# Local attention on one Trainium2 core: probabilities turned by VectorE in 32 by 32 blocks, the weighted state in four row groups of 32 keys, the previous key block by a shift in SBUF

## The chip, the cores and the metric

The kernel runs on one core of one Trainium2 chip. The metric is the device time of one execution in microseconds (us), as a median of several runs. Engines are named as in the profile: PE is TensorE (matrix products), PEld its weight loads, DVE is VectorE, ACT is ScalarE, POOL is GpSimd, and SP (SyncE) issues the DMAs. All data is float32.

## The reference

The reference is a two-block transformer on 16 sequences of 256 tokens and 128 channels. The change lies in one part of it: six layers of *local* attention with 16 heads of 64 channels, each followed by a gated feed-forward net (FFN). A window of 32 queries sees its own 32 keys and the 32 keys of the window before:

```python
def look(t):
    p = jnp.pad(t, ((0, 0), (0, 0), (1, 0), (0, 0), (0, 0)))
    return jnp.concatenate([p[:, :, :nw], p[:, :, 1:]], axis=3)
bk2, bv2 = (look(bk), look(bv))
...
sim = jnp.einsum('bhwie,bhwje->bhwij', bq, bk2) * QK_SCALE
sim = jnp.where(mask, -jnp.finfo(sim.dtype).max, sim)
attn = jax.nn.softmax(sim, -1)
out = jnp.einsum('bhwij,bhwje->bhwie', attn, bv2)
```

The keys before the first window are zeros and masked. Around it are a linear attention block ahead and a global attention block behind, which the change leaves alone.

## The kernel before, in words

The program has three stages. The first (linear attention) and the third (global attention) are not touched. The middle stage holds the six local layers; its first projection starts at 269 us, its first scores at 306 us, its last scores at 3444 us.

**Data.** Two sequences (512 tokens) make a *unit*; there are 8 units. The state of a unit lies with channels on partitions and tokens along the row (`zs`). The kernel does not form the values V: it weights the *state* by the probabilities (128 channels for every head) and then multiplies by the product of the V and output weights of that head (`wvo`). For that product the state must also lie with tokens on partitions: `upright` (L804) transposes it on PE, copies it on ACT (L813) and stores it to a DRAM buffer `rows` that has 32 zero rows ahead (L815); `windows` (L819) loads it back as `xw`, so that partitions 64·par to 64·par+63 hold the 64 keys of one window (L825, 8 loads for a unit).

**Steps.** The stage is one loop of 192 steps (`n`, L1065) and some more that drain it; step n handles two pairs of heads of one unit, so that a unit takes four steps, but each operation of a step belongs to an older step (its lag is in the code: scores `n - 4`, division `n - 5`, transposition `n - 6`, weighting `n - 9`, merging `n - 10`). The order of all instructions on PE, DVE, ACT and POOL is that of the Python program (`manual_schedule`, L1062): each engine works through its own list in that order. In a step, PE does in turn

1. `merging` (L942): 16 products of weighted state and `wvo`,
2. in odd steps a small transposition for key norms (L781, then DVE copies `rkT`, L783),
3. `flipped` (L902): 8 transpositions of the probabilities (L906); DVE copies each four of them from PSUM to `prT` (L911), so that keys lie on partitions,
4. in every fourth step `upright`, and parts of an FFN (`go_on(behind)`),
5. in even steps `norms_sum` (L729), whose result ACT copies (`n2`, L738),
6. `weighted` (L913): 8 products of `xw` (64 keys x 128 channels, held as weights) and `prT` (64 keys x 256 columns), in two rounds of two PSUM buffers; within a round two row groups of PE (partitions 0 to 63 and 64 to 127) work at once, each into a buffer of its own; DVE and ACT copy each buffer to `zx` (L934, L936),
7. `scores` (L858): 64 small products in 64 x 32 tiles, into separate `sim` buffers,
8. the projections (L705).

After the scores DVE finds row maxima (L870, L872), ACT computes 16 exponentials (L880) and puts the mask into the next `sim` buffers (L844), and DVE applies the rotary tables (L710, L713); POOL adds, scales and divides (L721, L802, L898).

**PSUM.** `bank()` (L58) hands out four buffers `mm` of one bank each, strictly in turn. So the first write to a buffer waits until the last reader of the *fourth buffer before it* is done. Projections, transpositions, norms, FFN parts and `weighted` all share this ring of four; `merging` and `scores` have their own.

**Four kinds of step.** Which FFN part falls into a step depends on n modulo 4:

- n = 4k, the *gate step*: `upright`, three gate products (L1004), their Gelu on ACT (L1006, with a table load), `norms_sum`; `weighted` does the last quarter of its unit.
- n = 4k+1, the *value step*: DVE adds the merged result to the state (L955), `rkT`, three value products (L1014) that DVE multiplies with the gates (L1018); `weighted` does the first quarter, which reads the `prT` that `flipped` finished in this same step.
- n = 4k+2, the *closing step*: the FFN's mean (L968), its output product (L1027), a row of small products (L977), `norms_sum`.
- n = 4k+3, the *plain step*: `rkT`, four transpositions (L994), which DVE multiplies in (L995, then L996).

Of the kernel before, what the change touches and what calls it, by code (L numbers as in the profile page):

```python
# [10 lines left out]
F32 = mybir.dt.float32  # L11
# [7 lines left out]
B, L, D = 16, 256, 128  # L19
NU = B // 2  # L20
U = 2 * L
DEPTH = 6
INNER = 1024
NP = INNER // 128
WIN = 32
# [19 lines left out]
def adaln_kernel(  # L45
# [25 lines left out]
    def work(tag, shape=(128, 512), bufs=None):  # L71
        if stage.get("flat"):
            t = stage["flat"].tile([128, 512], F32, tag="flat", name=tag)
            if len(shape) == 4:
                t = t.rearrange("p (a b c) -> p a b c", a=shape[1], b=shape[2])
            return t
        kw = {} if bufs is None else {"bufs": bufs}
        return stage["pool"].tile(list(shape), F32, tag=tag, name=tag, **kw)
# [521 lines left out]
    with ExitStack() as es:  # L600
# [24 lines left out]

        ks = [persistent(f"k{j}", (128, 2, PAD + L)) for j in range(8)]

        rows = [dr.tile([2, PAD + L, D], F32, tag=f"rows{j}", name=f"rows{j}") for j in range(2)]
        zero = work("zero")[0:PAD, 0:D]
        nc.vector.memset(zero, 0.0)  # L630
        for home in rows:
            for s in range(2):
                nc.sync.dma_start(home[s, 0:PAD, :], zero)
        rope = lc.tile([128, 2, 2, L], F32, tag="rope", name="rope")
        nc.sync.dma_start(rope, io["c_rope"].rearrange("p (j a) t -> p j a t", j=2))

# [164 lines left out]
            k = ks[m % 8][:, :, PAD:]  # L801
            nc.gpsimd.tensor_tensor(k, k, two(kn), ALU.mult)  # L802

        def upright(u, home):  # L804

            pt = bank()
            for t in range(4):
                s, c = t // 2, PAD + 128 * (t % 2)
                nc.tensor.transpose(
                    pt[:, t * 128 : (t + 1) * 128], zs[u][:, s, c : c + 128], ident  # L810
                )
            xt = work("xt").rearrange("p (s h d) -> p s h d", s=2, h=2)
            nc.scalar.copy(xt.rearrange("p s h d -> p (s h d)"), pt)  # L813
            for s in range(2):
                nc.sync.dma_start(  # L815
                    home[s, PAD : PAD + L, :].rearrange("(h p) d -> p h d", p=128), xt[:, s]
                )

        def windows(s, home):  # L819


            xw = atile("xw", (128, 8, 128))
            for r in range(0, 128, WIN):
                t0 = r % (2 * WIN)
                nc.sync.dma_start(  # L825
                    xw[r : r + WIN],
                    home[s, t0 : t0 + L, :].rearrange("(w p) d -> p w d", p=WIN),
                )
            return xw

# [66 lines left out]
                    prf, prf, rsum[:, x].unsqueeze(2).to_broadcast([128, 8, 64]), ALU.mult  # L899
                )  # L900

        def flipped(p, x, pr, prT):  # L902

            pt = bank()
            for st in range(4):
                nc.tensor.transpose(  # L906
                    pt[:, st * 128 : (st + 1) * 128],
                    pr[:, x, st].rearrange("p h k -> p (h k)"),
                    ident,
                )  # L910
            nc.vector.tensor_copy(prT[:, p + x, :], pt)  # L911

        def weighted(j, xw, prT):  # L913

            zx = atile("zx", (128, 2, NP, 128), 1)
            for k in (2 * j, 2 * j + 1):
                pz = [bank(), bank()]
                for w in range(2):
                    for par in range(2):
                        r = slice(64 * par, 64 * par + 64)  # L920
                        nc.tensor.matmul(  # L921
                            pz[par][:, w * 256 : (w + 1) * 256],
                            xw[r, (2 * k + w) % 8, :],
                            prT[r, :, 64 * k + 32 * w : 64 * k + 32 * w + 32],
                            start=True,
                            stop=True,
                            skip_group_check=True,
                        )
                for par in range(2):
                    c0 = 64 * (k % 2)  # L930
                    dst = zx[:, par, :, c0 : c0 + 64].rearrange("p a (w q) -> p w a q", w=2)
                    src = pz[par].rearrange("p (w a q) -> p w a q", w=2, a=NP)
                    if par:
                        nc.vector.tensor_copy(dst, src)  # L934
                    else:
                        nc.scalar.copy(dst, src)  # L936
            return zx

        def merging(j, zx, vo, py):
# [125 lines left out]
        while n < N + 10 or behind:  # L1065
# [19 lines left out]
            if 0 <= n - 6 < N:  # L1085
                i, u, p = place(n - 6)
                if p == 0:
                    prTs[i, u] = atile("prT", (128, NP, 512))
                pr = prs.pop(n - 6)
                for x in range(2):  # L1090
                    flipped(p, x, pr, prTs[i, u])
            for s, lag in ((0, 8), (1, 10)):
                v, r = divmod(n - lag, QS)
                if r == 0 and 0 <= v < DEPTH * NU:
                    if s == 0:
                        upright(v % NU, rows[v % 2])
                    xws[v, s] = windows(s, rows[v % 2])
            go_on(behind)
            if 0 <= n - 5 < N:
                divided(prs[n - 5], ssum)  # L1100
# [6 lines left out]
                n2 = norms_sum([squares.pop(m) for m in range(2 * n - 4, 2 * n)])  # L1107
            v, r = divmod(n - 9, QS)
            if 0 <= v < DEPTH * NU:
                zxs[v, r] = weighted(r, xws[v, r // 2], prTs[v // NU, v % NU])  # L1110
            go_on(behind)
            if sims:
                m = 2 * (n - 4)
# [506 lines left out]
```

## Time and profile before

| | |
|---|---|
| median of 3 runs | 4091.11 us (4088.63 to 4092.11) |
| span of the profiled execution | 4089.6 us, 1.5 us under the median |
| PE, DVE, ACT, POOL busy, share of the span | 94%, 72%, 68%, 65% |
| part of the middle stage, 306 to 1900 us: PE, DVE, ACT, POOL busy | 1507.7, 1197.6, 1153.0, 1137.1 of 1594 us |
| granted TensorE clock, 306 to 3460 us | 0.99 to 1.00 |
| median time from scores to scores, ending in the gate, value, closing, plain step | 17.69, 17.00, 17.75, 13.15 us |

The profile is one execution. Its groups give for each line of the program how often an operation ran, how long it was busy and what ended the idle time ahead of it; the chain of waits follows the end back from instruction to what released it; the timeline lists instructions in order. Busy time of PE is counted from start to modelled end, so neighbouring matrix products overlap in it, and a PE that is shown busy may still be waiting between two products. A float32 product is two records of PE ("x16" for 8 products), a transposition is one.

### The profile page before, as it was taken

The numbers are of one execution on the slowest core, as the hardware profiler recorded it, in microseconds if no ns is written. First come the engines' busy times: TensorE is split into PE (matmuls) and PEld (weight loads), VectorE is DVE, ScalarE is ACT, GpSimd is POOL, SyncE is SP. The second block draws the span as 40 slices with busy tenths as digits, with TensorE's granted clock in tenths as the row PEclk, the third lists the DMA queues.
The fourth block names the chain that finished last, engine by engine and source line by source line (L and its number), as shares of the span: only waits on it lengthen the run. The fifth ranks groups of instructions, "written<-read, shape, count | busy, mean of one in ns | idle before, by whom it ended". The sixth has DMA issues, their size and how long they took to land.

```text
span 4089.6 us, 117058 instructions
## 1 busy us (share of the span) xinstructions
PE 3824.8 (94%) x44534; PEld 2533.5 (62%) x44534; DVE 2944.4 (72%) x6006; ACT 2797.5 (68%) x9683; POOL 2653.6 (65%) x3374
## 2 busy tenths in 40 slices
PE   7877899999999999999999999999999999799998
PEld 4534666666666666666666666666666666455554
DVE  6756777777777777777777777777777775476664
ACT  4536777777777777677777777776777776366665
POOL 6437777767776777677776777777777665255453
PEclk9878999999999999999999999999999999899999
DMA  1334454445545445454554444454545443200000
GB/s 42 42 83 118 121 126 115 123 118 128 126 124 127 117 122 125 117 127 113 128 131 121 121 123 116 123 130 120 127 107 131 115 118 79 63 1 6 9 6 9
DMA packets 316617, 408.82 MB, mean 100 GB/s; under 512 B 48745, under 2 KB 212632, under 8 KB 316056
## 3 DMA queue, kind: packets, MB, share of 16 engines
q1 hardware_dynamic: 316056, 401.33, 39.6%
q8 instruction: 353, 5.78, 0.6%
q14 instruction: 208, 1.70, 0.1%
HBM read 178.26 MB, written 21.56 MB: 49 GB/s over the span
## 4 chain that ended last, share of the span: by engine, by line
PE 53%; DVE 16%; ACT 16%; issue 6%; POOL 5%; DMA 2%; SPq 1%; ACTq 0%; DVEq 0%; POOLq 0%
PE mm L921 8%; ACT pr L880 7%; PE y L942 6%; PE mm L705 6%; PE sim L858 6%; DVE sent L710 3%; PE mm L729 3%; PE mm L1027 3%; ACT sq L708 2%; PE mm L1014 2%; PE mm L1398 2%; DVE mx L870 2%; PE mm L906 2%; PE sim L1325 2%; DVE k L713 2%
## 5 line engine op out<-in xcount | busy, mean ns | idle before, releaser
L880 ACT ACTIVATE pr<-sim,nb,rq 128x64 f32<-128x64 f32 x3072 | 1229.2, 453 | 366.9 <-DVE nb L872 307.5
L880 ACT ACTIVATION_READ_ACCUMULATOR pr<-sim,nb,rq 128x1 f32 x3072 | 783.1, 255 | 0.0
L942 PEld LDWEIGHTS y<-zx,wvo 128*128 128x128 f32 x6144 | 715.8, 192 | 93.0 <-issue 88.3
L802 POOL TENSOR_TENSOR k<-k,kn 128x512 f32<-128x512 f32 x384 | 483.7, 1274 | 435.9 <-DMA kn<-rkh 434.4
L705 PE MATMUL mm<-z,wqk 128*128 128x512 f32 x1536 | 710.3, 604 | 13.4 <-DMA wqk<-in_L_ffn_Wqkv_dram 7.9
L942 PE MATMUL y<-zx,wvo 128*128 128x128 f32 x6144 | 717.9, 275 | 2.2 <-ACT zx L936 1.8
L721 POOL TENSOR_TENSOR q<-q,got 128x512 f32<-128x512 f32 x384 | 488.5, 1272 | 300.4 <-DMA got<-sent 173.2
L710 DVE SCALAR_TENSOR_TENSOR sent<-mm,vec,rope 128x512 f32<-128x512 f32 x768 | 571.0, 743 | 117.4 <-ACT sq L708 109.9
L934 DVE COPY zx<-mm 128x512 f32<-128x512 f32 x384 | 255.3, 674 | 375.0 <-PE mm L921 374.5
L708 ACT ACTIVATE sq<-mm 128x512 f32<-128x512 f32 x768 | 475.6, 619 | 30.9 <-PE mm L705 29.5
L721 POOL TENSOR_TENSOR k<-k,got 128x512 f32<-128x512 f32 x384 | 496.4, 1293 | 0.0
L705 PEld LDWEIGHTS mm<-z,wqk 128*128 128x128 f32 x1536 | 281.9, 192 | 328.5 <-issue 252.5
L921 PE MATMUL mm<-prT,xw 64*128 64x256 f32 x3072 | 452.5, 401 | 11.6 <-ACT n L738 6.4
L921 PEld LDWEIGHTS mm<-prT,xw 64*128 64x128 f32 x3072 | 326.7, 188 | 179.9 <-DVE rsum L893 38.6
L898 POOL TENSOR_TENSOR pr<-pr,rsum 128x512 f32<-128x512 f32 x384 | 392.3, 1043 | 14.0 <-PE mm L1004 7.4
L936 ACT COPY zx<-mm 128x512 f32<-128x512 f32 x384 | 227.0, 596 | 248.9 <-PE mm L921 248.4
L870 DVE TENSOR_REDUCE mx<-sim 128x8 f32<-128x512 f32 x384 | 263.1, 685 | 138.7 <-PE sim L858 137.9
L1368 POOL TENSOR_TENSOR pr<-pr,rsum 128x256 f32<-128x256 f32 (+1 forms) x256 | 205.1, 832 | 242.2 <-DVE rsum L1366 218.2
L858 PEld LDWEIGHTS sim<-k,q 64*32 64x32 f32 x24576 | 264.3, 106 | 80.9 <-issue 56.4
L858 PE MATMUL sim<-k,q 64*32 64x64 f32 x24576 | 299.5, 227 | 11.8 <-POOL k L802 6.5
L1354 ACT ACTIVATE pr<-lg,nm 128x128 f32<-128x128 f32 (+1 forms) x512 | 226.3, 443 | 117.3 <-DVE nm L1343 109.4
L713 DVE SCALAR_TENSOR_TENSOR q<-mm,vec,rope 128x512 f32<-128x512 f32 x384 | 284.5, 741 | 0.0
(253 smaller groups left out, 6244.7 us busy)
## 6 DMA issues: line engine op xcount, KB each, us to landing
got<-sent SPq DMA_DIRECT2D x1536, 128.0 KB
kn<-rkh SPq DMA_DIRECT2D x768, 128.0 KB
xw<-rows SPq DMA_DIRECT2D x384, 128.0 KB
rows<-xt SPq DMA_DIRECT2D x96, 128.0 KB
wqk<-in_L_ffn_Wqkv_dram SPq DMA_DIRECT2D x48, 128.0 KB
bhome<-brow SPq DMA_DIRECT2D x1, 3072.0 KB
wv<-in_L_ffn_Wqkv_dram SPq DMA_DIRECT2D x12, 256.0 KB
wo<-in_L_ffn_Wo_dram SPq DMA_DIRECT2D x12, 256.0 KB
```

What stands on the lines that cost most here:

```text
L705: nc.tensor.matmul(pp, wqk[:, j, :], xs, start=True, stop=True)
L708: nc.scalar.activation(sq, pp, AF.Square)
L710: nc.vector.scalar_tensor_tensor(two(sent[:, j, :]), two(pp), scale, tab[1], ALU.mult, ALU.mult)
L713: nc.vector.scalar_tensor_tensor(r, two(pp), scale, tab[0], ALU.mult, ALU.mult)
L721: nc.gpsimd.tensor_tensor(r, r, two(got[:, j, :]), ALU.add)
L802: nc.gpsimd.tensor_tensor(k, k, two(kn), ALU.mult)
L858: nc.tensor.matmul(sims[par][32 * c : 32 * c + 32, c0 : c0 + 64], q[r, s, t0 : t0 + 32], k[r, s, t0 : t0 + 64], start=False, stop=True, sk ...
L870: nc.vector.tensor_reduce(mx, sim.rearrange("p (b k) -> p b k", b=8), AX.X, ALU.max)
L880: nc.scalar.activation(pr[:, x, st, par, :], sims[par][:, b * 64 : (b + 1) * 64], AF.Exp, bias=nbs[par][:, b : b + 1], scale=rn[:, par, b ...
L898: nc.gpsimd.tensor_tensor(prf, prf, rsum[:, x].unsqueeze(2).to_broadcast([128, 8, 64]), ALU.mult)
L921: nc.tensor.matmul(pz[par][:, w * 256 : (w + 1) * 256], xw[r, (2 * k + w) % 8, :], prT[r, :, 64 * k + 32 * w : 64 * k + 32 * w + 32], star ...
L942: nc.tensor.matmul(py[:, j * 128 : (j + 1) * 128], vo[:, h, :], zx[:, h % 2, h // 2, :], start=(h == 0), stop=(h == 2 * NP - 1), skip_grou ...
```

## The change

The probabilities are no longer transposed on PE. One VectorE instruction turns the two pairs of a step at once, in blocks of 32 by 32, from SBUF to SBUF. In each block of 32 partitions the 32 queries of a window become 32 keys, either of the window's own block or of the block before. `weighted` therefore works on 32 keys at a time: four row groups (one for each window of a 128-token tile, c = 0 to 3), each with two products that are added up in PSUM (b = 0 the block before, b = 1 the own block), 128 channels by 512 columns. All four `mm` buffers are taken together, one for each row group. The number of products (8), of buffers taken (4) and of copies (4) in a step stays the same. The upright state stays in SBUF (`own`), and the block before is made by two DMAs from SBUF to SBUF that shift it by 32 partitions (`before`); the DRAM buffer with its 2 stores and 8 loads for a unit goes.

```diff
-        rows = [dr.tile([2, PAD + L, D], F32, tag=f"rows{j}", name=f"rows{j}") for j in range(2)]
-        zero = work("zero")[0:PAD, 0:D]
-        nc.vector.memset(zero, 0.0)
-        for home in rows:
-            for s in range(2):
-                nc.sync.dma_start(home[s, 0:PAD, :], zero)
+        own = [persistent(f"own{j}", (128, 4, D)) for j in range(2)]
+        before = [persistent(f"before{j}", (128, 4, D)) for j in range(2)]
...
-        def upright(u, home):
+        def upright(u, xw):
...
-            xt = work("xt").rearrange("p (s h d) -> p s h d", s=2, h=2)
-            nc.scalar.copy(xt.rearrange("p s h d -> p (s h d)"), pt)
-            for s in range(2):
-                nc.sync.dma_start(
-                    home[s, PAD : PAD + L, :].rearrange("(h p) d -> p h d", p=128), xt[:, s]
-                )
-
-        def windows(s, home):
-            xw = atile("xw", (128, 8, 128))
-            for r in range(0, 128, WIN):
-                t0 = r % (2 * WIN)
-                nc.sync.dma_start(
-                    xw[r : r + WIN],
-                    home[s, t0 : t0 + L, :].rearrange("(w p) d -> p w d", p=WIN),
-                )
-            return xw
+            prev, cur = xw
+            nc.scalar.copy(cur.rearrange("p t d -> p (t d)"), pt)
+            nc.sync.dma_start(prev[WIN:128], cur[0 : 128 - WIN])
+            nc.sync.dma_start(prev[0:WIN, 1:4:2], cur[128 - WIN : 128, 0:4:2])
...
-        def flipped(p, x, pr, prT):
-
-            pt = bank()
-            for st in range(4):
-                nc.tensor.transpose(
-                    pt[:, st * 128 : (st + 1) * 128],
-                    pr[:, x, st].rearrange("p h k -> p (h k)"),
-                    ident,
-                )
-            nc.vector.tensor_copy(prT[:, p + x, :], pt)
+        def flipped(p, pr, prT):
+            nc.vector.transpose(
+                prT[:, p : p + 2, :].rearrange("p a c -> p (a c)"),
+                pr.rearrange("p x t h k -> p (x t h k)"),
+            )
...
             zx = atile("zx", (128, 2, NP, 128), 1)
-            for k in (2 * j, 2 * j + 1):
-                pz = [bank(), bank()]
-                for w in range(2):
-                    for par in range(2):
-                        r = slice(64 * par, 64 * par + 64)
-                        nc.tensor.matmul(
-                            pz[par][:, w * 256 : (w + 1) * 256],
-                            xw[r, (2 * k + w) % 8, :],
-                            prT[r, :, 64 * k + 32 * w : 64 * k + 32 * w + 32],
...
-                for par in range(2):
-                    c0 = 64 * (k % 2)
-                    dst = zx[:, par, :, c0 : c0 + 64].rearrange("p a (w q) -> p w a q", w=2)
-                    src = pz[par].rearrange("p (w a q) -> p w a q", w=2, a=NP)
-                    if par:
-                        nc.vector.tensor_copy(dst, src)
-                    else:
-                        nc.scalar.copy(dst, src)
+            moving = prT.rearrange("p a (t h b q) -> p t b h a q", t=4, h=2, b=2)
+            pz = [bank() for _ in range(4)]
+            for b in range(2):
+                for c in range(4):
+                    r = slice(WIN * c, WIN * c + WIN)
+                    nc.tensor.matmul(
+                        pz[c], xw[b][r, j, :], moving[r, j, b], start=(b == 0), stop=(b == 1)
+                    )
+            for c in range(4):
+                dst = zx[:, :, :, WIN * c : WIN * c + WIN].rearrange("p h a q -> p (h a) q")
+                src = pz[c].rearrange("p (n q) -> p n q", q=WIN)
+                if c % 2:
+                    nc.vector.tensor_copy(dst, src)
+                else:
+                    nc.scalar.copy(dst, src)
             return zx
...
-                pr = prs.pop(n - 6)
-                for x in range(2):
-                    flipped(p, x, pr, prTs[i, u])
-            for s, lag in ((0, 8), (1, 10)):
-                v, r = divmod(n - lag, QS)
-                if r == 0 and 0 <= v < DEPTH * NU:
-                    if s == 0:
-                        upright(v % NU, rows[v % 2])
-                    xws[v, s] = windows(s, rows[v % 2])
+                flipped(p, prs.pop(n - 6), prTs[i, u])
+            v, r = divmod(n - 8, QS)
+            if r == 0 and 0 <= v < DEPTH * NU:
+                xws[v] = before[v % 2], own[v % 2]
+                upright(v % NU, xws[v])
```

More of the change, by code (lines that the diff above doesn't have):

```diff
@@ L913, in weighted @@
         def weighted(j, xw, prT):
             zx = atile("zx", (128, 2, NP, 128), 1)
-            for k in (2 * j, 2 * j + 1):
-                pz = [bank(), bank()]
-                for w in range(2):
-                    for par in range(2):
-                        r = slice(64 * par, 64 * par + 64)
-                        nc.tensor.matmul(
-                            pz[par][:, w * 256 : (w + 1) * 256],
-                            xw[r, (2 * k + w) % 8, :],
-                            prT[r, :, 64 * k + 32 * w : 64 * k + 32 * w + 32],
[L925 to L928, printed above, removed]
-                for par in range(2):
-                    c0 = 64 * (k % 2)
-                    dst = zx[:, par, :, c0 : c0 + 64].rearrange("p a (w q) -> p w a q", w=2)
-                    src = pz[par].rearrange("p (w a q) -> p w a q", w=2, a=NP)
-                    if par:
-                        nc.vector.tensor_copy(dst, src)
-                    else:
-                        nc.scalar.copy(dst, src)
+            moving = prT.rearrange("p a (t h b q) -> p t b h a q", t=4, h=2, b=2)
@@ L1109, in adaln_kernel @@
             if 0 <= v < DEPTH * NU:
-                zxs[v, r] = weighted(r, xws[v, r // 2], prTs[v // NU, v % NU])
+                zxs[v, r] = weighted(r, xws[v], prTs[v // NU, v % NU])
             go_on(behind)
```

## The prediction

> **What bounds the kernel now.** I read the head of the page first, then the chain of waits, then a four-step cycle of the middle stage on the timeline.
>
> ```profile
> PE 3824.8 (94%) x44534; PEld 2533.5 (62%) x44534; DVE 2944.4 (72%) x6006; ACT 2797.5 (68%) x9683; POOL 2653.6 (65%) x3374
> PE 53%; DVE 16%; ACT 16%; issue 6%; POOL 5%; DMA 2%; SPq 1%; ACTq 0%; DVEq 0%; POOLq 0%
> ```
>
> These two seem to say "PE". But a third of the chain runs over DVE and ACT, and the chain of one cycle (2000 to 2070 us) says where:
>
> ```profile
> 2013.96 1.28 ACT L1006
> 2015.25 1.83 ACT fg L1006 x3
> 2017.09 0.48 ACT sim L844
> 2017.57 0.52 ACT n L738
> 2018.14 1.13 PE mm L921 x6
> 2019.27 1.45 PE sim L858 x89
> ...
> 2031.18 0.29 DVE rkT L783
> 2031.52 1.98 PE mm L1014 x4
> 2033.50 2.44 PE mm L921 x16
> 2035.93 1.68 PE sim L858 x95
> ```
>
> In the gate step ACT decides (table load, three Gelu, mask, then the copy `n2`, L738), and PE's second round of `weighted` (L921) starts only when that copy has freed its PSUM buffer. In the value step DVE decides. The timeline has the same for all engines:
>
> ```profile
> 2017.50 0.59 ACT L738 COPY n<-mm 128x512 f32<-128x512 f32 x1
> 2018.14 1.13 PE L921 MATMUL mm<-prT,xw 64*128 64x256 f32 x6 [0.30 <-ACT n L738]
> 2019.19 1.48 PE L858 MATMUL sim<-k,q 64*32 64x64 f32 x128
> 2032.69 2.06 DVE L1018 SCALAR_TENSOR_TENSOR fg<-mm,vec,fg 128x512 f32<-128x512 f32 x3
> 2033.43 2.50 PE L921 MATMUL mm<-prT,xw 64*128 64x256 f32 x16
> 2035.86 1.75 PE L858 MATMUL sim<-k,q 64*32 64x64 f32 x128
> ```
>
> From the end of `n2` (2018.09) to the scores (2019.19) it is 1.10 us; from the end of the last DVE product (2034.75) to the scores (2035.86), 1.11. I read this pair of rows in 42 cycles: last release to scores, gate step (`n2`, L738) 1.11 to 1.21 in all 42; value step (L1018) 1.11 in 37; plain step (L995) 1.11 in 36. A distance that never varies is a tail behind a wait. So in three of four steps the release of the *last* of the four `mm` buffers sets the scores, and only the closing step is set by PE alone (scores 1.20 after `n2`, but `weighted` is also just as long as where it never waits).
>
> **Where the tail comes from.** The last buffer takes two products of 256 columns in one row group, four records. Record by record, undisturbed products of one row group start 0.216 us apart, and the other row group's start 7 ns after them, so row groups do work at once. The tail is 4 x 0.216 = 0.86, and 0.25 for the first weights and the change to the scores.
>
> **The change, part by part.**
>
> *PE transpositions go* (8 a step). The chain gives them 0.87 us a step:
>
> ```profile
> L906 PE MATMUL mm<-ident,pr 128*128 128x128 f32 x1536 | 208.4, 277 | 6.2 <-DVE q L713 5.1 <-DVE k L713 0.7
> ```
>
> ```profile
> 2045.68 0.87 PE mm L906 x8
> 2062.81 0.87 PE mm L906 x8
> ```
>
> That is up to 192 x 0.87 = 167 us, but only where PE sets the end. In gate, value and plain steps it comes to a buffer that is not free any earlier: what is late next is the same `n2`, the same third L1018, the same L995.
>
> *`weighted` itself.* As before 8 products, but 512 columns each in four row groups. A record of 512 columns takes 0.43 (L1027: 6 records in 2.58 on the chain). If four row groups work at once, the whole is 4 x 0.43 = 1.72, the same as 8 x 0.216 = 1.72 before. Not shown by this trace: four *row* groups. Nearest rows: four *column* groups of 512 columns in `norms_sum` (L729, 16 records in 1.85 = 0.116 each, so about four at once), and the scores (two row by four column groups). End below: no cost. End above: two at a time, as L921 now, 3.44. I take four at once, by L729.
>
> *The ring.* All four buffers are now written side by side, and each collects both its products, so that the last to come free holds up four records of 0.43 in its row group, not four of 0.216. The three others fill the wait with their b = 0 products but then stand behind the fourth in PE's order. The tail becomes 1.11 + 4 x (0.43 - 0.216) = 1.97: **+0.86 us wherever the last release decides.** I counted the ring anew without the two buffers of `flipped`: gate step upright, three gates, `n2`, W1 to W4, so W4 waits for `n2` as before; value step `rkT`, three values, W1 to W4, so W4 waits for the third L1018 as before; closing step W4 on `n2`; plain step `rkT`, L994, W1 to W4, so W4 waits for L995 as before. Behind the waiting W4 on PE stand the b = 1 products, then the scores, and for those DVE's maxima and all of ACT's exponentials wait.
>
> *DVE: one transposition for two copies.* It goes to the same place of DVE's order. Two copies take 1.27 to 1.28 (2031.39, L911 x2). No row has a transposition. Nearest rows:
>
> ```profile
> L911 DVE COPY prT<-mm 128x512 f32<-128x512 f32 x384 | 245.9, 679 | 18.9 <-PE mm L906 18.4
> L996 DVE TENSOR_SCALAR fx<-fx,vec 128x512 f32<-128x512 f32 x48 | 53.4, 1113 | 1.7
> L384 DVE TENSOR_REDUCE ve<-s 128x12 f32<-128x1536 f32 x8 | 13.9, 1742 | 1.1 <-POOL s L381 1.1
> ```
>
> L384 (1536 columns) against L870 (512 columns, 0.685) gives 1.03 ns a column, so 1024 columns take 1.21. L996, from SBUF to SBUF like the new instruction, ran from 0.545 to 1.628; twice that is 3.26, the end above; below I take 0.8 (0.545 and half of it again). I take 1.21, an estimate: -0.07 us in value and plain step, where `flipped` stands ahead of L1018 and L995 on DVE; nothing in gate and closing step, where DVE idles afterwards (the zx copies wait 374.5 us for L921).
>
> *Copies of `zx`*: as many and as wide; nothing. The last one (DVE, 0.67) ends under the scores (1.45). *DMA*: 10 transfers a unit through DRAM become 2 in SBUF. They are needed one step (over 13 us) later, and SP mostly waits (1205.6 us at L715 for DVE's `sent`). Fewer issues could bring POOL's key scaling forward, but the scores wait for it only 6.5 us in the whole run: 0 to -6.5, I take 0. Four memsets of POOL at the start, 0.57 each by L615: at most +2.3, under the weights' loads: 0.
>
> **The sum, over a cycle of four steps.** Gate +0.86 (42 of 42). Value (0.86 - 0.07) x 37/42 = +0.70. Plain 0.79 x 36/42 = +0.68. Closing: PE and with it `n2` come 0.87 earlier, but the tail behind `n2` goes from 1.20 to 1.97: -0.10. Together +2.14 x 48 cycles = +103 us. The profiled execution spans 4089.6 and lies 1.5 under the median, so 4091 + 103 = **4194 us**.
>
> A rule that speaks against the change: the Trainium skill, "TensorEngine Tiling (Array Packing)", Gotcha 1: PSUM Pressure, says that row tiles write to different PSUM banks, so more row tiles need more banks at a time. The rows agree: L921's two row groups use a buffer each and stop at the later one. Counting PE's work alone would give 4091 - 167 = 3924; with the rule it is the sum above. The other, on the unshown concurrency: "TensorE: Matmul & The Clock Gate", Measured speedup vs the span model, has 3.07 times for four row tiles of 512 columns. No run here shows it; by it a record costs 0.56 rather than 0.43, and the sum would be some 4 x 0.13 x 192 = 100 us higher.
>
> **Rivals.**
>
> 1. *PE is the bound after all, faster.* For: 94% busy, 53% of the chain. If the waits of W4 shrink with PE's arrival, each step loses 0.87: 4091 - 167 = 3924. If only the tail doesn't grow, the closing step's 48 x 0.87 = 42 remain: 4049. Against: the constant 1.11 on releases by ACT and DVE. It decides where PE's own work and not a release comes last; now that is so in the closing step and in 11 of the 126 others that I read.
> 2. *Four row groups don't work at once.* Two at a time: the tail becomes 1.11 - 0.86 + 6 x 0.43 = 2.83, so +1.7 in three steps, and the closing step +0.85 by PE: about 5.9 x 48 = 283, 4374. For: no row shows four. Against: L729.
> 3. *The transposition is slow*: two passes, or held up by POOL as L996 is. At 2.4 us two steps of four are 1.19 longer: 48 x 2.38 = 114, 4308. For: L996's spread. Against: nothing in the rows above 1.03 ns a column without such a hold.
> 4. *Nothing to measure*: a transposition at 0.8 (-40), and a few unbound steps that gain, against a tail half as costly: 4091.
>
> **How the numbers follow.** Forecast 0.62 (own range 4150 to 4250), rival 1 0.18, rival 2 0.07, rival 3 0.08, rival 4 0.05. The forecast is the likeliest, 4194. From 4060 to 4320 leaves out most of rival 1 (0.13) and rival 2 (0.07). A measurement tells apart about 0.2%, 8 us: faster 0.20, same 0.05, slower 0.75.
>
> **What would show it.** Right: L906 gone; from the last release to the scores 1.97 in place of 1.11; PE's idle time ahead of `weighted` up, its busy time down by some 200; gate, value and plain step 0.7 to 0.9 longer, the closing step about as long; the transposition near 1.2. Wrong: a tail still near 1.1 (rival 1); records of `weighted` in one row group over 0.43 apart (rival 2); a transposition over 2 us or with a wide spread (rival 3); scores that wait for POOL's keys more than now.

## The result and the profile after

The changed kernel takes **4258.86 us** (median of 4 runs, 4250.02 to 4274.34), the kernel before 4089.87 beside it (4 runs, 4086.94 to 4092.11): ratio 1.042, 95% interval 1.0397 to 1.0443, so 169 us slower. The forecast was 4194, its range 4060 to 4320; the forecast's own narrower range, 4150 to 4250, was just missed. The profiled execution spans 4258.9 us.

The head of the page after, with the chain's shares by engine and by line:

```profile
PE 3965.7 (93%) x42998; PEld 2363.4 (55%) x42998; DVE 2863.3 (67%) x5813; ACT 2791.2 (66%) x9683; POOL 2657.5 (62%) x3378
PE 51%; DVE 21%; ACT 17%; issue 6%; POOL 4%; DMA 1%; SPq 0%; ACTq 0%; POOLq 0%; DVEq 0%
```

PE issues 1536 records fewer, and its busy time is *up* by 141 us, not down by the 200 that the prediction named. So PE's work either takes longer or lies more spread out, with other work no longer over it. DVE's share of the chain went from 16 to 21%.

The chain of waits over one cycle, from the end of the plain step (2011) through the gate step's scores (2032) and the value step (2044 to 2053) into the closing step:

```profile
2011.61 0.58 DVE fx L969
2012.24 1.98 PE mm L901 x10
...
2032.42 1.45 PE sim L840 x89
...
2044.55 1.25 DVE prT L887
2045.85 5.24 PE mm L901 x16
2051.09 1.98 PE sim L840 x121
2053.07 2.00 PE mm L942 x2
```

In the plain step DVE's `fx` (L969) releases W4 (the last of the four buffers), and 1.98 us of `weighted` stand behind it on the chain (before, the tail was 1.11 in most cycles). In the value step `weighted` takes 5.24 us, the scores behind it 1.98 where the gate step's take 1.45, and the two records of L942 (the FFN's mean) take 2.00. The same two records on the chain before:

```profile
2037.62 1.05 PE mm L968 x2
```

So PE ran at half its speed from about 2048 to 2055. The timeline of PE says why:

```profile
2041.37 2.74 PE L988 MATMUL mm<-fx,w 128*128 128x512 f32 x6
2045.85 2.68 PE L901 MATMUL mm<-prT,before 32*128 32x512 f32 x7 [1.74 <-DVE prT L887]
2047.80 1.13 PE L901 MATMUL mm<-prT,own 32*128 32x512 f32 x3
2048.33 1.05 PE L901 MATMUL mm<-prT,before 32*128 32x512 f32 x1
2048.34 2.75 PE L901 MATMUL mm<-prT,own 32*128 32x512 f32 x5
2051.02 2.05 PE L840 MATMUL sim<-k,q 64*32 64x64 f32 x128
```

All three value products (L988) are done at 2044.11, since two buffers fewer stand ahead of them. Then PE waits 1.74 us for the transposition, and the first seven records of `weighted` run one row group (a quarter of the array) at a time, as DVE's three products free one buffer after the other. So from 2044.11 to 2047.80 the array is empty or a quarter full, and after that the records run 0.85 apart in one row group instead of 0.43. The granted clock of the same trace, in the 3.41 us ahead of the slow piece and in the piece (columns as below, the clock third from the end):

```profile
2044.90:2048.31 3.41, 2.46 (x10) 1.37 (x14) 3.00 (x5) 0.50 (x1) 3.21 (x4) 1.00 0.34 70
2048.31:2055.14 6.83, 6.83 (x141) 3.58 (x134) 3.04 (x7) 1.96 (x6) 5.37 (x5) 0.50 0.40 97
```

The granted clock over the same work, before and after (us, then busy time of PE, PEld, DVE, ACT, POOL, then the granted clock, DMA share and GB/s):

```profile
306.00:1900.00 1594.00, 1507.68 (x20319) 1031.23 (x20315) 1197.61 (x2034) 1153.03 (x4081) 1137.06 (x1457) 0.99 0.49 123
```

```profile
306.00:1980.00 1674.00, 1572.39 (x19536) 945.76 (x19531) 1162.09 (x1945) 1151.16 (x4083) 1144.40 (x1462) 0.94 0.41 102
```

In the clock's records it is granted whole or half, never between; from 300 to 3430 us it stands at half for 53 us before and for **366 us** after (there the middle stage runs on to 3605, with 20 us more). The expectations below have 61 and 218 us where this text has 53 and 208: those were counted on an axis that starts some 11 us ahead of the first instruction.

From 42 full cycles of each trace I read the period of each kind of step (mean, scores to scores, in us) and the tail (last release to scores):

| kernel | gate | value | closing | plain | half clock, 300 to 3430 | time |
|---|---|---|---|---|---|---|
| before | 17.87 | 17.08 | 17.89 | 13.25 | 53 | 4089.87 |
| after | 18.68 | 18.98 | 18.81 | 13.49 | 366 | 4258.86 |
| difference | +0.81 | +1.90 | +0.92 | +0.23 | | +169 |
| predicted | +0.86 | +0.70 | -0.10 | +0.68 | | +103 |

The differences sum to 3.86 a cycle, 162 of the 169 us in these 42 cycles. The tail is 1.96 us in 42 of 42 gate steps, 42 closing steps and 37 plain steps; in the value step its median is 3.76.

The transposition, by line (minimum, median and maximum of 192, in ns), and what the largest wait of POOL became:

```profile
L887 DVE STREAM_TRANSPOSE prT<-pr x192: 1222/1233/1247, 331.1 to 3631.3; 128x1024 f32<-128x1024 f32 x192
```

```profile
POOL q L717 <- DMA got<-sent: 590.8, 162, 11.1
```

POOL's wait for the key norms fell from 434.4 to 23 us, but its wait for the exchanged halves rose from 173.2 to 590.8: the wait moved within POOL, whose share of the chain went from 5 to 4%.

### The profile page after: what moved, and what is told of

The parts are those of the page before. It is cut to its first block, busy times and chain, and to the rows that moved or that the text cites. A ratio compares the mean times of both kernels' runs of the same rounds, so it can differ in the third digit from the quotient of the medians.

```text
span 4258.9 us, 113272 instructions
## 1 busy us (share of the span) xinstructions
PE 3965.7 (93%) x42998; PEld 2363.4 (55%) x42998; DVE 2863.3 (67%) x5813; ACT 2791.2 (66%) x9683; POOL 2657.5 (62%) x3378
## 2 busy tenths in 40 slices
DMA packets 195064, 356.57 MB, mean 84 GB/s; under 512 B 42538, under 2 KB 86489, under 8 KB 194521
## 4 chain that ended last, share of the span: by engine, by line
PE 51%; DVE 21%; ACT 17%; issue 6%; POOL 4%; DMA 1%; SPq 0%; ACTq 0%; POOLq 0%; DVEq 0%
PE mm L901 15%; ACT pr L862 9%; PE sim L840 7%; PE mm L701 5%; PE y L916 4%; DVE sent L706 4%; PE mm L1001 3%; DVE k L709 3%; DVE mx L852 3%; ACT sq L704 3%; PE mm L725 3%; DVE prT L887 2%; PE mm L1368 2%; DVE q L709 2%; PE mm L942 2%
## 5 line engine op out<-in xcount | busy, mean ns | idle before, releaser
L717 POOL TENSOR_TENSOR q<-q,got 128x512 f32<-128x512 f32 x384 | 487.5, 1269 | 714.5 <-DMA got<-sent 590.8
L862 ACT ACTIVATION_READ_ACCUMULATOR pr<-sim,nb,rq 128x1 f32 x3072 | 773.4, 252 | 0.0
L701 PE MATMUL mm<-z,wqk 128*128 128x512 f32 x1536 | 720.2, 613 | 7.6 <-DMA wqk<-in_L_ffn_Wqkv_dram 6.7
L908 DVE COPY zx<-mm 128x512 f32<-128x512 f32 x384 | 264.7, 691 | 556.6 <-PE mm L901 541.5
L901 PE MATMUL mm<-prT,before 32*128 32x512 f32 x1536 | 524.0, 698 | 106.0 <-DVE prT L887 66.7
L701 PEld LDWEIGHTS mm<-z,wqk 128*128 128x128 f32 x1536 | 294.6, 200 | 340.7 <-issue 275.2
L910 ACT COPY zx<-mm 128x512 f32<-128x512 f32 x384 | 209.7, 590 | 401.8 <-PE mm L901 401.6
L901 PE MATMUL mm<-prT,own 32*128 32x512 f32 x1536 | 437.3, 710 | 0.0
L901 PEld LDWEIGHTS mm<-prT,before 32*128 32x128 f32 x1536 | 177.9, 193 | 391.6 <-DVE prT L887 100.1
L840 PEld LDWEIGHTS sim<-k,q 64*32 64x32 f32 x24576 | 279.3, 114 | 187.5 <-POOL pr L880 81.7
L840 PE MATMUL sim<-k,q 64*32 64x64 f32 x24576 | 315.1, 244 | 12.2 <-POOL k L798 9.4
```

The source lines that it names most:

```text
L701: nc.tensor.matmul(pp, wqk[:, j, :], xs, start=True, stop=True)
L717: nc.gpsimd.tensor_tensor(r, r, two(got[:, j, :]), ALU.add)
L840: nc.tensor.matmul(sims[par][32 * c : 32 * c + 32, c0 : c0 + 64], q[r, s, t0 : t0 + 32], k[r, s, t0 : t0 + 64], start=False, stop=True, sk ...
L862: nc.scalar.activation(pr[:, x, st, par, :], sims[par][:, b * 64 : (b + 1) * 64], AF.Exp, bias=nbs[par][:, b : b + 1], scale=rn[:, par, b ...
L901: nc.tensor.matmul(pz[c], xw[b][r, j, :], moving[r, j, b], start=(b == 0), stop=(b == 1))
```

## The experiments

The theory after the result: *the tail costs what was predicted, and the rest is TensorE's clock, which falls in the value step because PE stands idle and then works at a quarter of its array ahead of the rest of `weighted`*. The rivals: the rest is a slower weighting in itself; or the transposition on DVE; or the shift over SP's queue. Each time stands beside runs of the kernel before on the same chip (4082.8 to 4085.7 us).

**flip_alone.** The kernel before with the transposition alone. The old weighting reads it, so the keys are not in their right places; the shapes and the number of its instructions are those of a kernel that has them right.

```diff
-            pt = bank()
-            for st in range(4):
-                nc.tensor.transpose(
...
-            nc.vector.tensor_copy(prT[:, p + x, :], pt)
+            nc.vector.transpose(
+                prT[:, p : p + 2, :].rearrange("p a c -> p (a c)"),
+                pr.rearrange("p x t h k -> p (x t h k)"),
+            )
```

> The kernel before with one part of the change alone: one VectorE transposition in 32 by 32 blocks in place of the 8 PE transpositions and 2 copies; the weighting still takes 64 keys in two row groups, so that its keys no longer stand where the weighting reads them (the layout of the probabilities is changed, the work is the same). By the sum of the prediction this part alone is worth 0 in the gate step, -0.05 us in value and plain step, -0.87 in the closing step: about -1.0 us x 48 = -47, some 4043 us. Theory A (the clock falls because PE stands idle ahead of the weighting in the value step, where it now waits for the transposition on VectorE): this kernel has that wait too, so the granted clock falls towards 0.94 and the time is over 4100 us. Theory B (the clock falls only because the four row groups start one after another): the clock stays near 0.98 and the time is near 4043. If PE were the bound everywhere: 4091 - 167 = 3924.

4145.35 us, ratio 1.0147 (1.0131 to 1.0162); 208 us at half clock. So the clock falls with the old weighting too, and the transposition alone, with eight PE instructions less in a step, loses 60 us. Periods: 18.79, 17.61, 17.46, 13.46. The closing step gains 0.43; the gate step's +0.92 was in neither theory, and it is taken up again below.

**weight_alone.** The kernel before with the four row groups alone; PE still transposes (the keys are not in their right places either).

```diff
-                for w in range(2):
-                    for par in range(2):
...
+            for b in range(2):
+                for c in range(4):
+                    r = slice(WIN * c, WIN * c + WIN)
+                    nc.tensor.matmul(
+                        pz[c], xw[r, (2 * j + b) % 8, :], moving[r, j, b], start=(b == 0), stop=(b == 1)
+                    )
```

> The kernel before with the other part alone: PE still transposes the probabilities and the state comes back through DRAM, but the weighting is done in four row groups of 32 partitions over four PSUM buffers (the operands have the right shapes and places, not the right keys). Tail theory: the distance from the last release to the scores is 1.96 us rather than 1.11 in gate, value and plain step and 1.96 rather than 1.20 in the closing step: about +3.3 us a cycle, 40 to 48 cycles, +130 to +160, 4220 to 4250 us, with the granted clock near 0.98, since the 8 PE transpositions still fill the wait. Rival (PE's work decides): the products take 1.72 us as before, no change, 4091 us.

4197.13 us, ratio 1.0267 (1.0252 to 1.0283), granted clock 0.981: 111 us for the tail without any loss of clock (38 us at half clock, none of it in the 42 cycles). The tail is 1.96 in 42, 37, 42 and 37 of 42 cycles of the four kinds. The mechanism is as expected, the size is below the 4220 to 4250 expected: the periods grew by 0.88, 0.50, 0.51 and 0.45, not by 0.85 each. Part of what is given back is seen at one small DVE product (last section).

**warm.** The changed kernel with two unread products of 512 columns between the value products and `weighted`, in value steps alone. Nothing else is different.

```diff
+            if r == 0 and 0 <= v < DEPTH * NU:
+                idle = psy.tile([128, 512], F32, tag="y", name="idle")
+                for _ in range(2):
+                    nc.tensor.matmul(two(idle), mean128, rope[:, 0], start=True, stop=True)
```

> The changed kernel with two products of 512 columns more ahead of the weighting in every value step, into the accumulator bank that is free there; nobody reads them. They only fill PE's wait of 1.7 us for the transposition. Clock theory: what lies beyond the predicted 103 us is the TensorE clock, which falls to half in value steps; with the wait filled the granted clock returns to about 0.98, the tail of the value step falls from 3.76 to about 1.96 us and the closing step from 18.8 to about 17.5: some -2.8 us x 48 = -135, near 4125 us. Rival (the value step is long because of the order of releases, whatever the clock): no gain, or up to +0.2 us x 48 = +10, 4259 to 4270 us.

4135.08 us, ratio 1.0123 (1.0106 to 1.014): **work was added to the engine that is busy 93% of the span, and some 120 us went** (169 over the kernel before became 49). Half clock: 58 us, as before. The timeline of PE in the same step:

```profile
2038.82 2.74 PE L988 MATMUL mm<-fx,w 128*128 128x512 f32 x6
2041.80 1.95 PE L1082 MATMUL idle<-rope,mean 128*128 128x512 f32 x4 [0.23 <-DVE z L929]
...
2045.78 1.44 PE L901 MATMUL mm<-prT,own 32*128 32x512 f32 x5
2047.15 1.48 PE L840 MATMUL sim<-k,q 64*32 64x64 f32 x128
```

The fillers take the place of the wait. The five last records take 1.44 instead of 2.75, the scores 1.48 instead of 2.05. Periods: 18.69, 17.67, 17.46, 13.47; the value step's tail is back at 1.96. Against the kernel before that is +0.82, +0.59, -0.43, +0.22: here the prediction's own terms can be read without the clock. weight_alone, with the same tail but PE's transpositions kept, stands at +111: with the clock held, the rest of the change is worth some 60 us, most of it in the closing step (+0.51 there, -0.43 here).

**dram_again.** The changed kernel with the round trip through DRAM: 2 stores and 8 loads for a unit in place of the two shifts.

```diff
-            nc.sync.dma_start(prev[WIN:128], cur[0 : 128 - WIN])
-            nc.sync.dma_start(prev[0:WIN, 1:4:2], cur[128 - WIN : 128, 0:4:2])
+            for s in range(2):
+                nc.sync.dma_start(
+                    home[s, PAD : PAD + L, :].rearrange("(h p) d -> p h d", p=128), xt[:, s]
+                )
...
+                    nc.sync.dma_start(
+                        tile_[r : r + 64, 2 * s : 2 * s + 2],
```

> The changed kernel with the state led through DRAM again: 2 stores and 8 loads a unit in place of the 2 shifts within SBUF, loaded at the same lags as before the change. Theory: the loads blocked the DMA queue ahead of the loads of the key norms, so POOL's waits for those (434 us before, 23 after) return, and with them 0.45 us in the plain step: +22 us, about 4280 us. Rival (as predicted, the shift is worth nothing): within 6.5 us of the changed kernel, 4253 to 4265 us.

4263.03 us, ratio 1.043 (1.0415 to 1.0446), which overlaps with the changed kernel's 1.0397 to 1.0443. The shift is worth nothing that can be measured, as predicted. POOL's wait for the key norms did not return either (26.7 us): the theory that the eight loads hold it up falls.

**last_half.** The changed kernel without the block-before product of the last row group (a part of the keys is left out for a quarter of the windows): one product of eight less, and two records instead of four behind the last release.

```diff
+                    if (b, c) == (0, 3):
+                        continue
```

> The changed kernel without one eighth of the weighting: the last row group (the last window of each 128 tokens) leaves out the block of keys before. The three other row groups do both products, so that the whole takes 1.72 us where nothing waits, as before; only what the last buffer collects is halved, from four records to two. Tail theory: from the last release to the scores 1.11 us rather than 1.96 in gate and plain step, the closing step 0.75 shorter, the value step 0.86 to 1.6 shorter: some -3.7 us x 45 = -165, near 4094 us, up to 4135 if POOL's work meets the small DVE products more often again. Rival (the length of the weighting as a whole decides): no change, 4259 us.

4092.32 us, ratio 1.0019 (1.0006 to 1.0031), median tail 1.10 to 1.20 in gate, closing and plain step; 161 us less over the kernel before than the changed kernel. So what stands behind the last release counts, out of proportion to its share of the work. Not all of the 161 is the tail: the half clock fell too, from 366 to 260 us. By warm, where 308 us less of half clock went with 120 us, an estimate for these 106 is some 40 us, and the tail has the other 120. No run takes the product from another row group, so that its place was what counted rests on the tail's size in weight_alone.

**after_swap** and **before_swap.** If the tail stands ahead of the scores, put the scores ahead of `weighted`: in both kernels `weighted` goes behind scores and maxima. The move changes the order alone, not what is computed.

```diff
-            v, r = divmod(n - 9, QS)
-            if 0 <= v < DEPTH * NU:
-                zxs[v, r] = weighted(r, xws[v], prTs[v // NU, v % NU])
...
                 nbs = [maxima(sims[par], rn[:, par]) for par in range(2)]
                 ssum = small("ssum", (128, 2, 4, 2))
+            v, r = divmod(n - 9, QS)
+            if 0 <= v < DEPTH * NU:
+                zxs[v, r] = weighted(r, xws[v], prTs[v // NU, v % NU])
```

> The changed kernel with one thing moved: the weighting with its copies is placed behind the scores and the maxima of the same step rather than ahead of them. Tail theory: the scores then wait for no release; the wait for the last buffer passes under the 1.45 us of scores, ACT's exponentials start earlier against everything else, and PE's own work (some 56 to 58 us a cycle of four steps, against 70 now) or ACT's becomes the bound: 3700 to 3850 us. Rival (the wait only moves: PE then stalls ahead of the projections, and ACT's copies of the weighted state stand ahead of its exponentials): no gain, 4200 us or more.

> The kernel before with the same move: the weighting behind scores and maxima. Tail theory: it gains too, since its tail of 1.11 us leaves the path, but as PE then sets the end, it keeps the 0.87 us of transpositions in each of 192 steps: 3870 to 3980 us, slower than the changed kernel with the same move by up to 167 us. Rival (the wait only moves): no gain, 4086 us or more, and the two moved kernels as far apart as now (4%).

after_swap: **3981.78 us**, ratio 0.9746 (0.9731 to 0.976), faster than both kernels, but far from the 3700 to 3850 expected. before_swap: 4073.19, ratio 0.9981 (0.9968 to 0.9993), where 3870 to 3980 was expected. The chain of after_swap, from a gate step's `norms_sum` through the next step:

```profile
2009.27 1.85 PE mm L725 x16
2011.12 1.52 PE sim L840 x92
2012.64 1.97 PE mm L901 x15
2014.61 0.57 ACT zx L910
```

The scores now follow `norms_sum` at once. PE makes 66% of the chain (51% in the changed kernel): now PE sets most of the time, and what interrupts it here is the ring again, one place later (the next product waits for ACT's copy of `zx`, L910). The move took both losses away at once, the tail and the clock (67 us at half clock, 3 of them in the 42 cycles); no run tells their shares in it apart. The expectations took the tail away and let nothing else be late next; that was the mistake as far as these runs show it.

**flip_warm.** flip_alone with the fillers of warm (not the right keys).

> The kernel before with VectorE's transposition alone (as flip_alone, keys not in their right place), and two unread products of 512 columns ahead of the weighting in each value step. flip_alone took 4145 us, at half clock for 218 us of its middle, with a median tail of 2.06 us in the value step. If its loss is the clock, which falls because PE stands idle until the transposed probabilities are there, then: granted clock 0.98, value tail back to 1.11 to 1.3 us, the half-clock time back to about 61 us, and 4145 less 50 to 100 = 4043 to 4090, so at or below the kernel before. If the value and gate steps are longer for another reason (the 1.23 us of the transposition itself on the path of each step), the fillers change nothing but the clock's record: 4130 to 4150.

4129.35 us, ratio 1.0111 (1.0091 to 1.0131): 16 less, not 50 to 100. The value step's tail is back at 1.11 (37 of 42) and its period fell from 17.61 to 17.20, but 152 us at half clock remain. What the value step gained (0.41) the gate step lost: 18.79 to 19.20, with 82 us of half clock in 42 gate periods against 51. The timeline of PE in a gate step of flip_alone shows what happens there:

```profile
2029.50 1.02 PE L1001 MATMUL mm<-fx,w 128*128 128x512 f32 x2
2033.05 2.74 PE L1001 MATMUL mm<-fx,w 128*128 128x512 f32 x4 [2.53 <-ACT xt L813]
```

The second gate product (L1001, the four records at 2033) waits for ACT's copy of `upright`, two buffers earlier and not four; PE stands still for 2.5 us. The buffers' addresses in the built programs show why: against what the section on the kernel before says, the four `mm` are *not* always handed out in turn; a buffer that is free early can come again early. In 30 of 46 gate steps of flip_alone and flip_warm the second gate product gets the buffer that `upright` has just used (7 of 46 in the kernel before, none in the changed kernel, warm, weight_alone or last_half). In both the buffers of `weighted` come out of turn as well, and the tail of the closing step is 1.97 in 32 of 42 cycles, where the kernel before has 1.21. So flip_alone had a second cause in it.

**flip_ring, flip_ring_warm, before_ring.** The same kernels with the four buffers as four tags, taken strictly in turn (the first two not with the right keys).

```diff
+        if "turn" in stage:
+            stage["turn"] = (stage["turn"] + 1) % 4
+            return stage["ps"].tile(
+                [128, 512], F32, tag=f"mm{stage['turn']}", name="mm", bufs=1
+            )
```

> As flip_alone (VectorE's transposition alone, old weighting, keys not in their right place), but the four mm buffers are handed out strictly in turn. In flip_alone the pool gave the second gate product of 29 of 48 gate steps the buffer that upright had just used, so that PE stood 2.5 us and the clock fell there too. If that is what made its gate step longer: gate step back from 18.79 to about 17.9 us, 48 x 0.9 = 43 less than 4145, so about 4100, with the half clock left in the value step alone. If the gate step is longer for the transposition's own sake, 4130 to 4150.

> flip_ring with two unread products of 512 columns ahead of the weighting in each value step (keys not in their right place). If what is then left of the transposition's loss is the clock that falls in the value step: no half clock in the steady cycles, value step near 17.0 us, 4100 less 20 to 50 = 4050 to 4080, so not above the kernel before, as a transposition of 1.23 us for two copies of 1.28 should be. If the transposition costs by itself, 4100.

> The kernel before with the four mm buffers strictly in turn. In 7 of its 48 gate steps the second gate product has upright's buffer too; at 1 us each that is 7 us: 4075 to 4085 beside 4084, hardly to be told from no change. It is the base for the two kernels with the same buffers.

before_ring 4078.62, ratio 0.9988 (0.9976 to 1.0), as expected. flip_ring 4118.39, ratio 1.0079 (1.0051 to 1.0108): 27 of the 43 expected. The gate step's median is back at 17.70 (mean 18.30) and the closing step's mean went from 17.46 to 16.85, its tail back at 1.21 in all 42; but the plain step grew from 13.46 to 14.03. flip_ring_warm 4090.48, ratio 1.0032 (1.0019 to 1.0045): the fillers are worth another 28, and the half clock of value and closing periods falls from 102 to 7 us in the 42 cycles. So of flip_alone's 67 us over before_ring (on two chips, the kernel before within 3 us), 27 go with the buffers, 28 with the clock that falls in the value step, and 12 remain where 0 to -30 was expected. Against before_ring its periods stand at +0.48, +0.15, -1.10 and +0.87: the closing step gains more than the 0.87 that PE's transpositions took, and the plain step and, in part, the gate step give it back. The chain of flip_ring_warm between closing and plain step:

```profile
2052.14 1.23 POOL k L727
...
2055.01 2.00 POOL pr L904 x2
...
2061.16 0.26 POOL rk L778
...
2061.79 0.28 DVE rkT L789
2062.07 1.15 DVE prT L911
```

From 2051 to 2061 the chain lies on POOL: rotation, FFN norm, division, then the square root of the key norms (`rk`). `rkT` waits for it, and the transposition stands behind `rkT` on DVE. POOL has 13% of this kernel's chain and 5% of the one before's. The reading is that a closing step that ends earlier meets a POOL that doesn't; no run with a shorter POOL tests it.

**before_swap_ring.** before_swap had the buffer out of turn in 35 of 46 gate steps; here all are in turn.

> before_swap (the kernel before with the weighting behind scores and maxima) with the mm buffers strictly in turn. In before_swap 35 of 48 gate steps gave the second gate product the buffer that upright had just used. If that wait took what the move should have brought (gate step 17.9 to 18.0 us there, as before the move): gate step 0.9 shorter, 48 x 0.9 = 43 less, about 4030, and the changed kernel with the same move (3982) leads by some 50 and not by 91. If PE's work with its eight transpositions sets the end of the moved kernel, as the reading of before_swap was: within 10 us of 4073.

4053.27 us, ratio 0.9917 (0.9901 to 0.9934): 20 less than before_swap, between the two expectations (about 4030; 4063 to 4083). It isn't the gate step that gained: its period went from 18.02 to 17.89, where 0.9 was expected, and in before_swap the second gate product started more than 0.1 us late in only 14 of 45 gate steps, by at most 0.6. The plain step went from 14.03 to 13.54, 20 us over the 42 cycles; why stays open (20 us of half clock went from it too). PE has 61% of its chain, 3% in its eight transpositions. Under the same move the changed kernel (3982, no second gate product out of turn) leads by some 71 us, across two chips whose runs of the kernel before agree within 1 us: **the change pays once its tail stands behind the scores.**

## Why the prediction was right, and where it failed

- *The tail, 1.11 to 1.97.* Right, with its size: 1.96 where the clock holds. weight_alone shows it alone (+111 us), last_half takes it away. It would have decided the sign alone; but flip_alone, without it, lost 60 us as well, by what the prediction did not have.
- *Four row groups at once, 0.43 a record.* Right by the tail: 1.96 = 0.25 + 4 x 0.43. Rival 2 (tail 2.83) fell. In the chain of after_swap shown above 15 of the 16 records take 1.97 in all. The Trainium skill's "TensorEngine Tiling (Array Packing)", Gotcha 1: PSUM Pressure, cited in the prediction, says that row tiles write to different PSUM banks; here the wait for the fourth of them decided. The 3.07 times of "TensorE: Matmul & The Clock Gate", Measured speedup vs the span model, did not show here: records of a row group stand 0.43 apart, not 0.56.
- *The transposition, 1.21.* Measured 1.233, spread 1.222 to 1.247, though 158 of the 192 lie beside one of POOL's tensor operations: rival 3 fell, and no hold by POOL shows.
- *Shift and copies at 0.* Right for the shift (dram_again; DMA packets went from 316617 to 195064, and the time did not follow). The copies of `zx` were not tested alone.
- *Gate +0.86.* Measured +0.81.
- *Value +0.70.* **This step failed: +1.90.** The prediction had `weighted` wait for the same third L1018 as before and took that wait to be free. It counted the ring anew without the two buffers of `flipped`, and did not see what follows from the count: the value products are no longer held up between them, run in one piece, and leave PE one long empty stretch ahead of `weighted`. The missing term is the clock, put at nothing without a word: 150 us of half clock fall into the 42 value periods and 151 into the closing periods behind them. With the clock held (warm) the value step is +0.59.
- *Closing -0.10.* Measured +0.92, with the clock held -0.43. It starts inside the half-clock piece (scores, L942); the working was right in kind, and the gain is larger.
- *Plain +0.68.* Measured +0.23, and +0.22 in warm. Mis-sized: the tail there is 1.96 in 37 of 42, but the last release comes 0.7 us earlier than before, counted from the scores before. The shorter `nb` of the next section bears on it, 0.33 a step; a run for this alone was not made.
- *The sum.* Without the clock the prediction was too high by 54 (warm: +49 against +103), and it had no term for the clock, some 120 us. The two errors had opposite signs, and that 4194 lies within 66 us of 4259 is partly luck.
- *Rival 1 (PE is the bound).* As a forecast it fell (3924 or 4049). But the closing step, which the prediction too left to PE, gained more than the 0.87 reckoned (-1.10 in flip_ring_warm), and with the tail out of the way PE sets most of the time (66% of the chain of after_swap).
- *The sign to watch, PE's busy time down by some 200.* It went up by 141 us. With the clock held (warm) it is up by 69, of which the fillers are some 94 (48 x 1.95, an estimate): a fall of some 25 without them, far from 200.
- *The buffers in turn.* The reading that the four buffers come strictly in turn, on which the count of the ring rests, is not exact. For the gate products of the changed kernel it held in all 46 steps.

## What to carry to other kernels

Look for what stands *behind* the last release of a ring, not at the work of the stage: spreading the same products over more buffers doubled that stretch, and taking away an eighth of the products at its end was worth 161 us, part of it by the clock. An instruction that leaves a busy engine leaves a gap, and it is the gap that has to be priced, for the clock above all. A stage whose results are needed a step later belongs behind the one that feeds the critical chain; only then did the removed work pay here.

## What the runs showed of the hardware

- **The clock falls without a long idle stretch.** PE waited at most 1.74 us in the value step, followed by some 1.9 us at a quarter of the array; that halved its clock, 366 us in sum from 300 to 3430 us. The Trainium skill, "TensorE: Matmul & The Clock Gate", What's actually happening, asks for an idle window of about 3.4 us. The pieces at half clock here are 3.41 us or multiples of it, which agrees. That the window must be idle does not: ahead of the 42 falls in the changed kernel's cycles PE was idle for 0.43 to 1.73 of the 3.41 us (median 1.59). The measurement decides: a window in which the array is partly filled counted too. How empty a window must be, these runs do not settle.
- The clock's records and the instructions' agree in time: of the 38 pairs of neighbouring records of 512 columns that flip_alone ran about 0.85 apart, 36 lie within its half-clock pieces.
- **A tiny DVE product waits for POOL.** `nb` (128 x 8) has two inputs in SBUF. By line (minimum, median, maximum in ns), before and after:

```profile
L872 DVE SCALAR_TENSOR_TENSOR nb<-mx,rq x384: 166/365/1320, 308.5 to 3447.6; 128x8 f32<-128x8 f32 x192
```

```profile
L854 DVE SCALAR_TENSOR_TENSOR nb<-mx,rq x384: 166/168/1218, 308.5 to 3609.5; 128x8 f32<-128x8 f32 x192
```

  Where one of POOL's tensor operations lies beside it, it takes 540 ns in the mean (290 of 384), elsewhere 167. The Trainium skill, "SBUF — State Buffer", Two separate sides, has such a pair exclude each other, and these rows agree. In the changed kernel POOL is more often done by then (171 of 384 beside it): 63.6 us less in sum, 0.33 a step on the way to the exponentials. It looks as if a longer step bought back a part of itself; no run shows it alone.
